# A decoder layer on one core: separate tiles for the raw weights of the first batch, and feed-forward weights and residual rows issued on GpSimd's queue

## The chip, the core and the metric

The kernel runs on one core of a Trainium2 chip. The core has a matrix engine (TensorE, PE), a vector engine (VectorE, DVE), an activation engine (ScalarE, ACT), a general engine (GpSimd, POOL) and SyncE (SP), which here only issues DMAs. Each engine works through its own instructions in order and waits on semaphores for the others. A DMA is issued by an engine and is in that engine's order: what stands behind an issue that waits, waits too. Data lie in SBUF (128 partitions), sums of matmuls in eight PSUM banks, inputs and outputs in DRAM. The metric is the device time of one launch in microseconds (us); the median of the runs is what counts. One further execution was recorded by the hardware profiler.

## The reference: what is computed

One pre-norm decoder layer in fp32, with batch B = 4, T = 512 rows and D = 512 columns: attention with 16 heads of 128, cross attention with a given context, and a feed-forward part of width 1365 with ternary weights. Cut to what matters:

```python
# attention: x is the normed input; att mixes the 128 features of a head
q = (x @ Wq + bq).reshape(Bx, Tx, N_Q, N_HEADS)      # k, v in the same way
q = jnp.transpose(q, (0, 3, 2, 1))
k = jnp.transpose(k, (0, 3, 1, 2))
v = jnp.transpose(v, (0, 3, 2, 1))
att = jax.nn.softmax(q @ k / math.sqrt(N_K), axis=-1)
y = jnp.transpose(att @ v, (0, 2, 1, 3)).reshape(Bx, -1, N_V * N_HEADS)
x_1 = x_0 + y @ Wo + bo
# cross attention: 8 heads of 64 rows, keys and values are the context
x_2 = x_1 + gamma * (softmax(q_heads^T k_heads * scale) applied to v_heads)
# feed-forward, w1, w3, w2 replaced by ternary values
s = jnp.mean(jnp.abs(w)); q = jnp.clip(jnp.round(w / s), -1.0, 1.0) * s
x_3 = x_2 + (silu(n @ w1q.T) * (n @ w3q.T)) @ w2q.T
```

The product `q @ k` contracts over the 512 rows, so a head's scores are a 128x128 matrix.

## The kernel before

**Algebra and stages.** The scores are formed from the Gram matrix G of the normed input (`gram_upper`, `pg`), so that per head only products of 512x512 matrices with weights are left. The 16 heads fall into HG = 4 rounds j of NG = 4 heads. In a round, `u` is the input times a quarter of Wo (matmuls `pu`), `y` is G times Wk (`py`), `m` is Wv times `u` (`pm`), and `scores` makes `sc` from `y` and Wq, its row maximum `nmax` on DVE, and `e`, the softmax numerators, on ACT. `e` is scaled on DVE, turned by PE in the next round (`pe`, `turned`), multiplied with `m` (`po`, `output`) and added to four accumulators `acc`, which hold the residual rows. After round 3 these are stored to DRAM as `x_a`.

There are three stages. The first batch (lines 671 to 743) loads the raw weights from the inputs. The loop over batches 1 to 3 (752 to 778) does the same with weights that the first batch has prepared. The feed-forward stage follows (795 to 889).

**Exact products.** A matmul in plain fp32 is one path (`products_f32`). The other (`products`) splits both operands into a high part `h`, a low part `l` and a difference `d` (three tiles, called Tri) and sums a chain of `h` and `l` products and a chain of `d` products; the two PSUM banks are joined on DVE by `total`. In the first batch, `FIRST` says from which round on a kind of weight uses the split path: `o` from 2, `k` from 1, `v` never.

**Weights of the first batch.** `first_weights(n, j, ...)` loads, for a kind n of `o`, `k`, `v`, `q` and a round j, four raw chunks of 128x512 (256 KB each) on SP, and for `k`, `v`, `q` one tile `last`; DVE then gates each chunk in place (a bias row is put in by a small DMA on POOL). The gate is a number made from an earlier result (`gate_of`), so that the order of the work is kept. `keep_weights` makes the parts on DVE (`h` at line 253, `l` at 255, `d` at 258) and stores each part to DRAM (`kept`, line 244) by a DMA on POOL's queue. Raw chunks of `o` and `q` share the tag `raw` with 7 buffers; raw chunks of `k` and `v` and all parts of `o` lie in the pool `a_w` with 18 buffers; the parts of `k` and `v` share `part` with 12.

**Weights of the later batches.** `weights(n, b, j)` loads the kept parts on SP into the same pool `a_w`. In batch 1 a part `d` that was not kept is made on DVE and stored on POOL. The pool `a_w` is open from the start, beside the pool `first`; the pools of the cross attention (`c_x`, `c_in`, `c_p`, `c_pt`) are opened after `first` is closed and lie in its space.

**Side work.** While PE works through the rounds of batches 1 to 3, two generators give out one step at a time at each `tick`. `cross` does the cross attention of the batch before: it reads `x_a` back (`cs` for the moments, `cx` for the values), loads `keys`, and stores `x_c`; its DMAs are on SP, those of the last batch on POOL. `quantize` does the ternary weights: it loads 35 pieces (`abs`, up to 128x512) into the pool `a_stage` of two buffers and sums their absolute values on DVE (line 498), and later loads the same pieces again (`tern`), makes ternary values and stores them to DRAM as `t_w`. For all of this, `staged` and the store at line 525 use `load`, which is SP's queue. At the end of round 3 of the first batch the two stage buffers are held (`held_0`, `held_1`, line 740) until the first two `y` of that round are there.

**What sets the order.** The program text does not fix the order of an engine's instructions: a scheduler places them engine by engine. So where a DMA stands on its queue, and where a reduce stands on DVE, follow from the scheduler and from which buffers come free when. DMAs of a queue take eight semaphores in turn.

Of the kernel before, what the change touches and what calls it, by code (L numbers as in the profile page):

```python
# [37 lines left out]
def decoder_layer_kernel(  # L38
# [91 lines left out]
    def apool(name, bufs):  # L130
        return apools.enter_context(tc.tile_pool(name=name, bufs=bufs))

    x3p, xnp, g3p, u3p, wp = (
        apool("a_x3", 12), apool("a_xn", 4), apool("a_g3", 1), apool("a_u3", 12), apool("a_w", 18)
    )
    yp, stp, tp = apool("a_y", 5), apool("a_stage", 2), apool("a_t", 3)
    ep, mp, accp = apool("a_e", 1), apool("a_m", 4), apool("a_acc", 4)
    bo_bc = g3p.tile([P, D], F32, name="bo_bc")
# [39 lines left out]
    def load(dst, src):  # L178
        nc.sync.dma_start(dst, src)
        return dst  # L180

    def wtile(name, dt=F32R):
        return wp.tile([P, GW], dt, tag="w", name=name)

    w_of = {"q": wq, "k": wk, "v": wv}

    def heads(t):
# [23 lines left out]
    def first_weights(n, j, first, gate):  # L211

        if n != "o":
            last = first.tile([P, GW], F32, tag="last", bufs=2, name=f"{n}_last_{j}")
            load(heads(last), of_heads(w_of[n][:, D - 1 : D, :], j).to_broadcast([P, NG, DH]))
        chunks = []
        for k in range(KC):
            name = f"{n}_raw_{j}_{k}"
            if n in "oq":
                t = first.tile([P, GW], F32, tag="raw", bufs=7, name=name)  # L220
            else:
                t = wtile(name, F32)
            if n == "o":
                load(t, by_group(wo[j * T : (j + 1) * T, :], k))
            else:
                load(heads(t), of_heads(w_of[n][:, ts(k, P), :], j))
                nc.vector.scalar_tensor_tensor(t, t, gate[0], last, ALU.mult, ALU.subtract)
                if k == KC - 1:
                    bias = bqkv[:, ts(KINDS.index(n), GW)].rearrange("(o g) c -> g o c", o=1)
                    nc.gpsimd.dma_start(heads(t[P - 1 :, :]), of_heads(bias, j))  # L230
            chunks.append(t)
        return chunks

    def keep_weights(n, j, chunks, first, gate):


        def part(p, k):
            name = f"{n}_{p}_{j}_{k}"
            if n == "o":
                return wtile(name)  # L240
            return first.tile([P, GW], F32R, tag="part", bufs=12, name=name)

        def keep(name, tile):
            nc.gpsimd.dma_start(name[ts(k, P), :], tile)

        tris = []
        for k, t in enumerate(chunks):
            if n == "q":
                keep(kept_q[j], t)
                continue  # L250
            tri = Tri(part("h", k), part("l", k), part("d", k) if exact(n, 0, j) else None)
            h, l = tri.h.bitcast(F32), tri.l.bitcast(F32)
            nc.vector.tensor_scalar(tri.h, t, gate[1], None, ALU.mult)
            keep(kept[n, j, "h"], h)
            nc.vector.scalar_tensor_tensor(tri.l, h, -S, t, ALU.mult, ALU.add)
            keep(kept[n, j, "l"], l)
            if tri.d is not None:
                nc.vector.tensor_tensor(tri.d, l, h, ALU.subtract)
                keep(kept[n, j, "d"], tri.d.bitcast(F32))
            tris.append(tri)  # L260
        return tris

    def weights(n, b, j):
        if n == "q":
            return [load(wtile(f"q_{b}_{j}_{k}", F32), kept_q[j][ts(k, P), :]) for k in range(KC)]
        tris = []
        for k in range(KC):
            tri = Tri(*(wtile(f"{n}{p}_{b}_{j}_{k}") for p in "hld"))
            make = b == 1 and not exact(n, 0, j)
            for p in "hl" if make else "hld":  # L270
                load(getattr(tri, p).bitcast(F32), kept[n, j, p][ts(k, P), :])
            if make:
                nc.vector.tensor_tensor(
                    tri.d, tri.l.bitcast(F32), tri.h.bitcast(F32), ALU.subtract
                )
# [187 lines left out]
    def output(b, j, eT, ms, accs):  # L463
        for g in range(NG):
            po = bank(f"po_{b}_{j}_{g}")
            nc.tensor.matmul(po, lhsT=eT[:, g, :], rhs=ms[g], start=True, stop=True)  # L466
            scale = (S if exact("o", b, j) else 1.0) * (S if exact("v", b, j) else 1.0)
            nc.vector.scalar_tensor_tensor(accs[g], po, scale, accs[g], ALU.mult, ALU.add)  # L468
            if j == HG - 1:
                (nc.gpsimd if b == B - 1 else nc.sync).dma_start(by_group(x_a[b], g), accs[g])  # L470


    third = (HID + 2) // 3
# [9 lines left out]

    def staged(src, name):
        r, n = src.shape
        return load(stp.tile([P, 512], F32, tag="stage", name=name)[:r, :n], src)

    def quantize_steps(name):

# [27 lines left out]
        for i, (src, t) in enumerate(pieces):  # L517
            piece = staged(src, f"tern_{name}_{i}")
            r, n = t.shape
            above = stp.tile([P, 512], BF16, tag="above", name=f"above_{name}_{i}")  # L520
            nc.vector.tensor_scalar(above[:r, :n], piece, s[:r, 0:1], None, ALU.is_gt)
            nc.vector.scalar_tensor_tensor(
                piece, piece, s[:r, 1:2], above[:r, :n], ALU.is_lt, ALU.subtract
            )
            load(t, piece)
            yield

    def quantize():
# [142 lines left out]
    for j in range(HG):  # L671
# [77 lines left out]
        cpools.enter_context(tc.tile_pool(name=n, bufs=k, side="right"))  # L749
        for n, k in (("c_x", 3), ("c_in", 2), ("c_p", 4), ("c_pt", 2))  # L750
    ]
    for b in range(1, B):
        G = gram_upper(b, xs)
        waiting[2] = turned(*waiting[:3])
        output(*waiting)
        side = Side(cross(b - 1, *cpool), CROSS_STEPS, TICKS + 6)

        def tick():
            quant.tick()
            side.tick()  # L760

        g3 = gram_rest(b, G)
        for j in range(HG):
            u3 = values_out(b, j, x3, weights("o", b, j), tick)
            if j > 0:
                waiting[2] = turned(*waiting[:3])
            ys = keys_of(b, j, g3, weights("k", b, j), tick)
# [7 lines left out]
            ms = values_of(b, j, weights("v", b, j), u3, tick)  # L775
            e = scores(b, j, weights("q", b, j), ys)
            waiting = [b, j, e, ms, accs]
        side.rest()
    waiting[2] = turned(*waiting[:3])
    output(*waiting)  # L780
    quant.rest()
    apools.close()


# [151 lines left out]
```

## Time and profile before

| what | us |
| --- | --- |
| median of 3 runs | 1235.23 (1233.06 to 1236.63) |
| the profiled execution | 1231.67 |
| its span, first to last instruction | 1229.4 |
| PE busy | 1184.3 |
| DVE busy | 777.5 |
| ACT busy | 448.5 |
| POOL busy | 140.9 |
| end of `sc` of round 3 of the first batch, from the span's start | 215.4 |
| mean granted clock of PE | 0.992 of full |

The profile has a page and views that can be asked for. The page gives busy times and, in 40 slices of the span, the busy tenths of each engine (9 is 90% or more), PE's granted clock in tenths, and the share in which the 16 DMA engines were busy. The view of waits lists, for an engine, the line and tile that waited, what released it, the total in us, how often, and the longest. The timeline gives start, duration, engine, line, operation, output<-input, and in brackets the idle time before with its releaser. The view by stretches gives each engine's busy time in a window with the count of instructions in brackets, then the granted clock, the DMA share and GB/s. SPq and POOLq are the DMA issues of SP and POOL. DMA issues with their time from issue to landing:

```profile
kept_kh<-k_h POOLq DMA_DIRECT2D x16, 256.0 KB, 6.6
kept_vh<-v_h POOLq DMA_DIRECT2D x16, 256.0 KB, 5.0
kept_q<-q_raw POOLq DMA_DIRECT2D x16, 256.0 KB, 2.9
k_raw<-in_wk_dram SPq DMA_DIRECT2D x16, 256.0 KB, 8.3
v_raw<-in_wv_dram SPq DMA_DIRECT2D x16, 256.0 KB, 6.5
abs_w<-in_w1t_dram SPq DMA_DIRECT2D x12, 227.5 KB, 3.5
abs_w<-in_w3t_dram SPq DMA_DIRECT2D x12, 227.5 KB, 5.1
x_a<-acc SPq DMA_DIRECT2D x12, 256.0 KB, 2.5
keys<-in_kv_dram POOLq DMA_DIRECT2D x4, 256.0 KB, 3.3
x_a<-acc POOLq DMA_DIRECT2D x4, 256.0 KB, 4.2
cs<-x_a POOLq DMA_DIRECT2D x4, 256.0 KB, 3.0
```

The last column is the median time from issue to landing in us; the rows on POOL for `keys`, `x_a` and `cs` are those of the last batch.

### The profile page before, as it was taken

How to read it: one execution, taken by the hardware profiler on the slowest of the kernel's cores; microseconds unless marked ns; L12 is line 12 of the kernel's file. 1: busy time of each engine (PE TensorE's matmuls, PEld its weight loads, DVE VectorE, ACT ScalarE, POOL GpSimd, SP SyncE). 2: the span in 40 equal slices, each digit the busy share in tenths (PEclk: the TensorE clock that was granted, in tenths of full speed). 3: DMA queues.
4: the chain of work that ended last, by engine and by line, in shares of the span. 5: the costliest groups of instructions: out<-in, count | busy, mean ns of one | idle time of the engine just before them, and what ended most of it. 6: DMA issues, size and time to landing. Idle time of an engine off the chain costs nothing.

```text
span 1229.4 us, 15851 instructions
## 1 busy us (share of the span) xinstructions
PE 1184.3 (96%) x5262; PEld 825.7 (67%) x5262; DVE 777.5 (63%) x1579; ACT 448.5 (36%) x946; POOL 140.9 (11%) x238
## 2 busy tenths in 40 slices
PE   7999889889999999999999999999999999999998
PEld 3456565567776666777676677777667766678786
DVE  6866958587586856666677557485847835634232
ACT  2221212235242433433343334243445826823020
POOL 2533533120000001000000010000001000000000
PEclk9999999889999999999999999999999999999999
DMA  9799897786778686866787696677963120030101
GB/s 286 269 314 319 299 297 258 226 281 228 241 239 286 203 299 232 282 214 231 241 297 243 211 318 226 214 273 266 342 231 113 43 94 9 9 106 6 61 9 52
DMA packets 154137, 257.20 MB, mean 209 GB/s; under 512 B 16068, under 2 KB 59124, under 8 KB 154056
## 3 DMA queue, kind: packets, MB, share of 16 engines
q1 hardware_dynamic: 139272, 208.97, 51.6%
q0 software_dynamic: 14784, 47.22, 10.2%
q8 instruction: 42, 0.69, 0.2%
q14 instruction: 39, 0.32, 0.1%
HBM read 193.22 MB, written 62.91 MB: 208 GB/s over the span
## 4 chain that ended last, share of the span: by engine, by line
PE 80%; DMA 8%; DVE 4%; issue 4%; POOL 1%; ACT 1%; SPq 1%; POOLq 0%; DVEq 0%; ACTq 0%
PE h L851 13%; PE y L878 7%; PE xs L575 5%; PE xo L619 5%; PE xp L106 4%; PE sc L429 4%; PE po L466 4%; PE pg L361 2%; PE pm L320 2%; PE pu L320 1%; PE py_1d L299 1%; PE py_3d L299 1%; DMA abs_w<-in_w1t_dram 1%; PE py L320 1%; PE py_1h L288 1%
## 5 line engine op out<-in xcount | busy, mean ns | idle before, releaser
L851 PE MATMUL h<-fxh,t 128*128 128x512 f32 (+1 forms) x352 | 140.5, 401 | 0.8 <-ACT fxh L116 0.8
L851 PE MATMUL h<-fxl,t 128*128 128x512 f32 (+1 forms) x352 | 138.3, 395 | 0.0
L587 ACT ACTIVATE p<-xs,xnmax 128x512 f32<-128x512 f32 x128 | 87.0, 687 | 80.6 <-DVE xnmax L582 41.3
L581 DVE TENSOR_REDUCE xnmax<-xs 128x1 f32<-128x512 f32 x128 | 84.1, 685 | 30.6 <-PE xs L575 30.6
L851 PEld LDWEIGHTS h<-fxh,t 128*128 128x128 f32 (+1 forms) x352 | 65.1, 185 | 20.0 <-issue 1.5
L851 PEld LDWEIGHTS h<-fxl,t 128*128 128x128 f32 (+1 forms) x352 | 65.1, 185 | 15.7
L575 PE MATMUL xs<-keys,qs 64*128 64x512 f32 x256 | 73.0, 641 | 1.3 <-DVE m L308 1.3
L878 PE MATMUL y<-t,gh 128*128 128x512 f32 (+1 forms) x176 | 69.5, 395 | 0.0
L878 PE MATMUL y<-t,gl 128*128 128x512 f32 (+1 forms) x176 | 68.9, 391 | 0.0
L106 PEld LDWEIGHTS xp<-ident,p 128*128 128x128 f32 x512 | 58.8, 140 | 13.2 <-issue 3.0
L106 PE MATMUL xp<-ident,p 128*128 128x128 f32 x512 | 66.5, 273 | 0.8 <-DVE u L308 0.8
L619 PE MATMUL xo<-pt,vals 128*64 128x512 f32 x256 | 63.3, 599 | 2.4 <-ACT pt L109 2.4
L862 DVE SCALAR_TENSOR_TENSOR gf<-h,scales_w,sl 128x512 f32<-128x512 f32 (+1 forms) x44 | 32.9, 748 | 48.3 <-PE h L851 39.9
L109 ACT COPY pt<-xp 128x512 f32<-128x512 f32 x96 | 53.4, 594 | 26.5 <-PE xp L106 26.5
L466 PE MATMUL po<-m,eT 128*128 128x512 f32 x128 | 60.3, 615 | 2.7 <-ACT eT L109 2.7
L599 DVE TENSOR_SCALAR p<-p,xrden 128x512 f32<-128x512 f32 x128 | 56.4, 483 | 3.3
L320 PE MATMUL pm<-u,v_raw 128*128 128x512 f32 x128 | 55.6, 592 | 0.0
L663 POOL TENSOR_TENSOR acc<-acc,bo_bc 128x512 f32<-128x512 f32 x16 | 21.1, 1338 | 289.9 <-DMA acc<-in_x_dram 238.6
L860 ACT ACTIVATE sl<-h,scales_w 128x512 f32<-128x512 f32 (+1 forms) x44 | 30.2, 688 | 63.1 <-PE h L851 62.9
L468 DVE SCALAR_TENSOR_TENSOR acc<-po,acc 128x512 f32<-128x512 f32 x64 | 42.6, 687 | 15.6 <-PE po L466 15.4
L442 ACT ACTIVATE e<-sc,nmax 128x128 f32<-128x128 f32 x64 | 22.7, 369 | 79.8 <-DVE nmax L438 79.8
L171 ACT ACTIVATE uh<-u 128x512 fp32r<-128x512 f32 x48 | 30.4, 633 | 49.9 <-DVE u L308 49.7
(262 smaller groups left out, 2545.5 us busy)
## 6 DMA issues: line engine op xcount, KB each, us to landing
oh<-kept_oh SPq DMA_DIRECT2D x48, 256.0 KB, 4.7
ol<-kept_ol SPq DMA_DIRECT2D x48, 256.0 KB, 5.0
kh<-kept_kh SPq DMA_DIRECT2D x48, 256.0 KB, 5.0
kl<-kept_kl SPq DMA_DIRECT2D x48, 256.0 KB, 4.7
vh<-kept_vh SPq DMA_DIRECT2D x48, 256.0 KB, 4.5
vl<-kept_vl SPq DMA_DIRECT2D x48, 256.0 KB, 5.1
q<-kept_q SPq DMA_DIRECT2D x48, 256.0 KB, 5.2
kd<-kept_kd SPq DMA_DIRECT2D x44, 256.0 KB, 4.8
```

Source lines behind the costliest of these rows:

```text
L106: nc.tensor.transpose(pt[:, ts(k, P)], src[:, ts(k, P)], ident)
L109: nc.scalar.copy(dst, pv)
L320: nc.tensor.matmul(p, lhsT=lhs(k)[:, ts(i, P)], rhs=rhs(k), start=(k == 0), stop=(k == 3))
L429: nc.tensor.matmul(sc[:, ts(g, DH)], lhsT=w[k][:, ts(g, DH)], rhs=ys[k][:, ts(g, DH)], start=(k == 0), stop=(k == KC - 1),)
L466: nc.tensor.matmul(po, lhsT=eT[:, g, :], rhs=ms[g], start=True, stop=True)
L575: nc.tensor.matmul(sc, lhsT=qs[rows, ts(m, P)], rhs=keys[rows, :], start=True, stop=True)
L581: nc.vector.reduce_max(nmax[:, j : j + 1], scs[j], axis=AX.X)
L587: nc.scalar.activation(p, scs[j], AF.Exp, bias=nmax[:, j : j + 1], scale=xscale, accum_out=den[:, j : j + 1],)
L599: nc.vector.tensor_scalar(ps[j], ps[j], rden[:, j : j + 1], None, ALU.mult)
L619: nc.tensor.matmul(po[rows, :], lhsT=vals[:, l, rows], rhs=pt[j][:, l, :], start=(l == 0), stop=(l == NC - 1),)
L851: nc.tensor.matmul(ph[:r, :], lhsT=t[:, k, i * P : i * P + r], rhs=fxT[j][:, k, :], start=(k == 0 and j == 0), stop=(k == KC - 1 and j == 1),)
L878: nc.tensor.matmul(py, lhsT=g[i][j][:r, ts(c, P)], rhs=t2[:r, i, :], start=(i == 0 and j == 0), stop=(i == NHC - 1 and j == 1),)
```

## The change

Three things are changed. The raw chunks of the first batch get a tag for each kind with four buffers (16 in all), `last` has three buffers, and the parts get places by kind: exact `o` parts `h` and `l` go to the pool `a_u3`, exact `o` parts `d` to four tiles `od`, all parts of `v` to four tiles `vpart`, and `part` with its 12 tiles is left to `k` and to the `o` parts of the first two rounds. The pool `a_w` is opened only after `first` is closed and after the pools of the cross attention, on the right side, with waits for each tile instead of for the whole pool, and is closed before the other pools of attention. And 117 DMAs go from SP's queue to POOL's: the 70 loads of `staged`, the 35 stores of ternary values, and the 12 stores of `x_a` of batches 0 to 2 (those of batch 3 were on POOL before).

```diff
-    x3p, xnp, g3p, u3p, wp = (
-        apool("a_x3", 12), apool("a_xn", 4), apool("a_g3", 1), apool("a_u3", 12), apool("a_w", 18)
-    )
+    x3p, xnp, g3p, u3p = apool("a_x3", 12), apool("a_xn", 4), apool("a_g3", 1), apool("a_u3", 12)
...
-            last = first.tile([P, GW], F32, tag="last", bufs=2, name=f"{n}_last_{j}")
+            last = first.tile([P, GW], F32, tag="last", bufs=3, name=f"{n}_last_{j}")
...
-            if n in "oq":
-                t = first.tile([P, GW], F32, tag="raw", bufs=7, name=name)
-            else:
-                t = wtile(name, F32)
+            t = first.tile([P, GW], F32, tag=f"raw_{n}", bufs=4, name=name)
...
-            if n == "o":
-                return wtile(name)
-            return first.tile([P, GW], F32R, tag="part", bufs=12, name=name)
+            if n == "o" and exact(n, 0, j):
+                if p != "d":
+                    return u3p.tile([P, D], F32R, tag="u3", name=name)
+                tag, bufs = "od", 4
+            else:
+                tag, bufs = ("vpart", 4) if n == "v" else ("part", 12)
+            return first.tile([P, GW], F32R, tag=tag, bufs=bufs, name=name)
...
-    def weights(n, b, j):
+    def weights(n, b, j, wp):
+        def wtile(name, dt=F32R):
+            return wp.tile([P, GW], dt, tag="w", name=name)
...
-                (nc.gpsimd if b == B - 1 else nc.sync).dma_start(by_group(x_a[b], g), accs[g])
+                nc.gpsimd.dma_start(by_group(x_a[b], g), accs[g])
...
     def staged(src, name):
         r, n = src.shape
-        return load(stp.tile([P, 512], F32, tag="stage", name=name)[:r, :n], src)
+        piece = stp.tile([P, 512], F32, tag="stage", name=name)[:r, :n]
+        nc.gpsimd.dma_start(piece, src)
+        return piece
...
-            load(t, piece)
+            nc.gpsimd.dma_start(t, piece)
...
+    wpools = ExitStack()
+    wp = wpools.enter_context(tc.tile_pool(name="a_w", bufs=18, side="right", reuse_waits="tile"))
     for b in range(1, B):
...
-            u3 = values_out(b, j, x3, weights("o", b, j), tick)
+            u3 = values_out(b, j, x3, weights("o", b, j, wp), tick)
...
+    wpools.close()
     apools.close()
```

More of the change, by code (lines that the diff above doesn't have):

```diff
@@ L180, in load @@
         return dst
-    def wtile(name, dt=F32R):
-        return wp.tile([P, GW], dt, tag="w", name=name)
     w_of = {"q": wq, "k": wk, "v": wv}
@@ L763, in decoder_layer_kernel @@
         for j in range(HG):
-            u3 = values_out(b, j, x3, weights("o", b, j), tick)
+            u3 = values_out(b, j, x3, weights("o", b, j, wp), tick)
             if j > 0:
                 waiting[2] = turned(*waiting[:3])
-            ys = keys_of(b, j, g3, weights("k", b, j), tick)
+            ys = keys_of(b, j, g3, weights("k", b, j, wp), tick)
             if j > 0:
@@ L774, in decoder_layer_kernel @@
                 x3 = parts_of(b + 1, xs)
-            ms = values_of(b, j, weights("v", b, j), u3, tick)
-            e = scores(b, j, weights("q", b, j), ys)
+            ms = values_of(b, j, weights("v", b, j, wp), u3, tick)
+            e = scores(b, j, weights("q", b, j, wp), ys)
             waiting = [b, j, e, ms, accs]
```

## The prediction

> **What bounds the kernel now.** I read the page first, to see whether any engine is the bound.
>
> ```profile
> span 1229.4 us, 15851 instructions
> PE 1184.3 (96%) x5262; PEld 825.7 (67%) x5262; DVE 777.5 (63%) x1579; ACT 448.5 (36%) x946; POOL 140.9 (11%) x238
> PE   7999889889999999999999999999999999999998
> PEclk9999999889999999999999999999999999999999
> DMA  9799897786778686866787696677963120030101
> ```
>
> TensorE (PE) is busy 96%: 45 us of idle time is all that better overlap could remove, plus what a lowered clock costs. Both lie in the first quarter: from slice 10 (about 310 us) PE shows 9 throughout and the clock is full. So the table of PE's waits comes next.
>
> ```profile
> PE pg L361 <- DVE xn L338: 8.7, 1, 8.7
> PE pu_2d L299 <- ACT e L442: 5.2, 1, 5.2
> PE py_0h L287 <- DMA kh<-kept_kh: 4.6, 4, 2.2
> PE pe L106 <- DVE e L453: 4.3, 2, 3.3
> PE pu_3d L299 <- ACT e L442: 3.3, 1, 3.3
> ```
>
> The first line is the start and stays. The two `pu` lines belong to the first batch; I look up what made `e` late there in the timeline.
>
> ```profile
> 119.22 0.75 DVE L227 SCALAR_TENSOR_TENSOR k_raw<-k_raw,gate,k_last 128x512 f32<-128x512 f32 x1 [7.72 <-DMA k_raw<-in_wk_dram]
> ...
> 123.84 0.68 DVE L437 TENSOR_REDUCE nmax<-sc 128x4 f32<-128x512 f32 x1
> ...
> 128.13 3.24 PE L299 MATMUL pu_2d<-o_d,xd 128*128 128x512 f32 x7 [5.20 <-ACT e L442]
> ...
> 166.39 0.75 DVE L227 SCALAR_TENSOR_TENSOR k_raw<-k_raw,gate,k_last 128x512 f32<-128x512 f32 x1 [9.31 <-DMA k_raw<-in_wk_dram]
> ...
> 174.41 0.68 DVE L437 TENSOR_REDUCE nmax<-sc 128x4 f32<-128x512 f32 x1
> ```
>
> The scores `sc` were done at 113.6 (start 109.87, 3.73 long), but their maximum `nmax` ran at 123.84: it stands on VectorE (DVE) behind work on `k_raw`, and DVE idled 7.72 us for that load. `e` frees the PSUM bank that `pu_2d` waits for. In round j=3 the same happens with 9.31 us. The `k_raw` issues begin at 110.28 and 156.85, behind other kinds of weight on SP's queue. The third place is the transition to batch 1:
>
> ```profile
> 224.33 0.68 DVE L437 TENSOR_REDUCE nmax<-sc 128x4 f32<-128x512 f32 x1
> ...
> 227.49 1.08 PE L106 MATMUL pe<-ident,e 128*128 128x128 f32 x4 [3.33 <-DVE e L453]
> ```
>
> Here ten reduces of `abs_w` stand before `nmax`, and their loads come in pairs, since the stage pool has two buffers. Last, the table by stretches (the figure after POOL is the granted clock):
>
> ```profile
> 120.00:130.00 10.00, 4.80 (x17) 3.58 (x17) 8.68 (x19) 4.24 (x12) 3.40 (x7) 0.89 0.75 237
> 220.00:230.00 10.00, 5.95 (x26) 4.33 (x25) 4.62 (x15) 3.91 (x14) 0.54 (x1) 0.83 0.71 223
> 250.00:260.00 10.00, 7.30 (x18) 4.94 (x19) 9.69 (x19) 4.51 (x8) 2.17 (x3) 0.70 0.72 235
> ```
>
> Each stall is followed by a lowered clock. A stretch of 10 us at clock c loses 10(1−c).
>
> **First batch: raw tiles per kind.** Stalls between the start and 215.4 (end of `sc` of j=3) sum to 12.4 us: 5.2 + 3.3, and 3.9 in small ones of the same table cut to this stretch (0.9 for `k_l`, 0.9 for `u`, 0.8 for `gate` and four below 0.6), most of them again for parts of `k`, which come earlier now. The clock lost 1.1 (0.89) + 0.6 (0.94) + 0.5 (0.95) + 1.2 (0.88) = 3.4 us.
> - j=2 and j=3: in the new instruction order `k_raw` of the next round is issued as soon as its own four tiles are read, half a round early, so DVE no longer idles for it. What `nmax` stands behind is then `v_raw`, whose load waits for the previous `pm`, done about 110; it lands 6.5 us after issue, 116. Then `nmax` at about 117 instead of 123.84, `e` at about 121 (3.4 us of table load and four exponentials, as at 125.28 to 127.96), and PE wants the bank at 122.9 (128.13 − 5.20). Gain 5.2. In j=3 `nmax` falls from 174.41 to about 162: gain 3.3.
> - j=1 pays. Two `k_raw` loads for j=2 stand on SP ahead of `v_raw` for j=1, and wait for the parts of `k`; `v_raw` is issued about 69, lands about 76, and `nmax`, at 64.51 before, goes behind four `v_raw` operations (4 × 0.75) to about 77, `e` to about 81. PE wants that bank at about 82. Margin 1 us; from there each us late is a us of stall. I take 1 us of stall, bounds 0 and 5 (the j=2 stall moved here).
> - `v` now has 4 part tiles for 8 parts: the fifth waits for the store of the first, 5.0 us (row of `kept_vh` on POOL). DVE is in order, so `q_raw` and `nmax` would be queued behind it; the totals of `u` and the scaling of `e` lie between and cover it. Bounds 0 and 8 us over four rounds (four times the 5.0 less 3 us of such work).
> - The extra `last` tile and `o` parts in other pools cost nothing by themselves: the waits on them were on tiles read 40 us earlier.
> - Bytes: 57.9 MB in 200 us before, DMA share 0.86 on average. About 2 MB of batch 1's first weights go later; 55.9 MB in 184 us is 304 GB/s, and at the 335 GB/s per full share seen (288/0.86) a share of 0.91. Stretches of 10 us at 1.03 and 1.07 occur before (80 to 90, 110 to 120), so it fits, but queueing returns some of the gain: I take 1 us, bounds 0 and 6.
>
> First batch: 12.4 + 3.4 − 1 − 1 = 13.8, so 14 us gained; with all bad bounds (5 + 8 + 6) it is 3 us lost.
>
> **Transition: feed-forward weights on POOL, weight pool opened later.** 117 DMAs leave SP (70 loads, 35 stores, 12 residual stores). On SP they cost issue time of 0.33 to 0.44 us each, about 45 us over 1000 us of a queue that isn't the bound; on POOL 0.54 us each, 63 us on an engine busy 140.9. The gain sought is that weights no longer queue behind a stalled `abs_w`. But `keys` of the cross attention now stands on SP ahead of six of the eight `oh`/`ol` loads, and waits for the whole first pool, to T0 (end of `sc` j=3). After T0 there are 8.9 (`pg`) + 5 (`pe`, `po`, `gt`) us of PE work before the first `pu`, then 11.2 us of it; the last `oh`/`ol` pair waits for `pg`'s reads, is issued at about T0+10, lands 5 us later, and is wanted at T0+18 (after those 13.9 and the stall of 4.1 below). Covered, by 3 us; without that stall it would wait about 1 us itself.
> - All 12 `abs_w` reduces now stand ahead of `nmax`, ten before. The first pair is free to load 19 us before T0 (its tiles are held until `y` of j=3 is copied, 196.22 before, with T0 at 215.4). Six pairs, each a landing L and 1.4 us of reduces, then 3.8 us for `nmax`, `e` and its scaling; PE asks at T0+8.9. The stall is 6(L+1.4) + 3.8 − 19 − 8.9 = 6L − 15.7. POOL never loaded `abs_w`: its nearest rows are `keys` 3.3, `cs` 3.0, `cx` 2.9 (quiet queues) and, upwards, `kept_kh` 6.6 in the busy first batch. I take 3.3, the same shape from an input: 4.1 us, against 3.33 + 0.72 = 4.05 now. Bounds 2.9 (1.7 us) and 6.6 (23.9 us).
> - `kh` loads: still behind `cs` and `cx`, which now wait for a POOL store of 4.2 us instead of 2.5; but fewer transfers stand on SP. I estimate 3 us of stall against 4.1. Net gain of the transition: 1 us; bounds +6 and −20.
>
> The page "SBUF — State Buffer" of the Trainium skill (section "SBUF: two separate sides") says that a GpSimd DMA waits for descriptors while DVE runs in a fast two-port mode, 620 ns becoming 3100. This speaks against the move. The trace has stores on POOL of 5.0 to 6.6 us among DVE work and 2.9 for `kept_q`, which is compatible. By the page, 2.5 us more for six pairs would add about 15 us; the rows I use come from the feed-forward stage, where DVE is less busy, so they say little on this.
>
> **Later batches and feed-forward.** From 320 us to the end all stalls of PE together are about 13 us, 1.6 of them from DMAs; the queue move can win at most that. It can lose where `cs` waits for a residual row on POOL behind feed-forward pieces and holds weights: covered by 18 weight buffers; 0, bounds +1.6 and −5.
>
> **Sum.** 14 + 1 + 0 = 15 us: span 1229.4 to 1214.4. The profiled run took 1231.67 (2.3 around the span), 3.6 below the median of 1235.23; taken off the median, 1220.
>
> **Rivals.**
> A. *The stalls only move.* `v_raw` becomes what `k_raw` was, `v`'s four tiles serialize DVE, and the queues are full at 0.91. For it: the 1 us margin in j=1. Against: the wait for `v_raw` before was 1.31 us in j=2. Price: the 5 us of j=1, 4 of the 8 for `v`, 3 of queueing out of 16: gain 4, time 1231.
> B. *The `abs_w` chain on POOL becomes the wait at the transition.* Place: DVE's queue ahead of `nmax` of j=3. It eats the other gains from 6L − 15.7 = 4.05 + 15, L = 5.8. For it: all twelve reduces are ahead, only two buffers, POOL rows of 5 to 6.6 in the first batch, and `abs_w` of w3 took 5.1 even on SP. Against: SP stands still at `keys` in that stretch, so the chain has the DMA engines nearly alone. At L = 8.3 (the slowest row, `k_raw`) the stall is 34, less 4 now, less the 14 and 2 us of other gains: 14 slower, 1249.
> C. *It doesn't do what it says:* SP is held at `keys` instead, and weights arrive as late as before while the first batch stays DMA-bound. 1235.
>
> **How the numbers follow.** Forecast 0.55, A 0.15, B 0.27, C 0.03. About 0.3% (3.7 us) is what a measurement of this kernel tells from no change. Faster: 0.55 and 0.09 of A; same: 0.06 of A and 0.02 of C; slower: the rest, 0.28. The forecast's own range is 1208 (all stalls and 6 us of the transition gone, and a little of the lowered clock) to 1229. The wide range reaches into B as far as 1246, with 1 in 10 beyond it and 1 in 10 below 1208.
>
> **What would show it.** Right: no wait of `pu_2d` and `pu_3d` on `e`, no idle DVE before `k_raw` in j=2 and j=3, `sc` of j=3 ending about 201, a clock over 0.95 in the first batch. Wrong: a new wait of `py_1d` on `e`, DVE idle before `v_h` on a `kept_vh` store, or `pe` waiting more than 10 us with `abs_w` landings over 5 us on POOL. A new stall of `pu_0` on `oh` would say that `keys` holds SP longer than I read it.

## The result, and the profile after

The changed kernel takes 1298.18 us in the median (1295.5 to 1300.71), against 1234.61 for the kernel before in the same comparison: a ratio of 1.0514, with an interval of 1.0486 to 1.0541. The prediction was 1220 us, with a range up to 1246. The change is slower by 63.6 us, more than the 14 us at which rival B, the slow one, was priced.

The profiled execution took 1297.42 us. First the page of the changed kernel: busy times, then the busy tenths of PE and its clock in 40 slices.

```profile
span 1295.6 us, 15874 instructions
PE 1209.5 (93%) x5262; PEld 837.3 (65%) x5262; DVE 779.9 (60%) x1579; ACT 448.7 (35%) x946; POOL 208.8 (16%) x355
PE   7989899799978999997889999997998899999998
PEclk9998899999989999998989999998999899999999
```

PE does the same 5262 matmuls, yet it is idle for 86.1 us (1295.6 − 1209.5) where it was idle for 45.1, and busy for 25 us more: the lowered clock now also shows in slices 12, 19, 21, 28 and 32, counted from 1 (from about 356 us on). Before, everything from slice 11 on was full. So the loss isn't in the first batch and the transition, where I had looked for gains and losses, but later. The ends of the `sc` groups on the timelines cut the span into three stages:

| stage | before | after | difference |
| --- | --- | --- | --- |
| first batch: start to the end of `sc` of round 3 | 215.5 | 217.9 | +2.4 |
| batches 1 to 3: from there to the end of the last `sc` | 691.9 | 745.5 | +53.6 |
| feed-forward stage: the rest | 322.0 | 332.2 | +10.2 |

The view of waits for PE in the changed kernel (total, times, longest):

```profile
PE po L465 <- DVE y L307: 15.9, 3, 7.2
PE py_2h L286 <- DVE u L307: 10.4, 2, 7.3
PE xs L576 <- ACT e L441: 9.1, 2, 4.6
...
PE xs L576 <- DVE qs L100: 8.2, 1, 8.2
PE pu_2d L298 <- DVE v_l L251: 5.7, 1, 5.7
...
PE pe L106 <- DVE e L452: 2.6, 2, 1.7
PE py_1d L298 <- ACT e L441: 2.6, 1, 2.6
```

`pu_3d` on `e` (3.3 before) is gone from the table, as predicted; `pe` has fallen to 2.6, where the prediction kept it at 4.1. The first three lines are new (`py_2h` on `u` was 0.4), and lie mostly in batches 1 to 3.

The view of waits cut to batches 1 to 3 says which way the loss goes. The last row sums PE's waits during which DVE itself stood for the load of a feed-forward piece; load_sp is the run below with the pieces' loads back on SP.

| PE in batches 1 to 3, us | before | changed | load_sp |
| --- | --- | --- | --- |
| idle until a DMA landed | 5.5 | 5.4 | 6.5 |
| idle until DVE or ACT was done | 10.0 | 42.9 | 7.8 |
| of these, while DVE stood for a piece | 5.6 | 33.2 | 0.3 |

So PE waits for weights no longer than before. What grew, by 32.9 us, is its waiting for DVE and ACT, and seven waits with DVE standing for a piece make up 33.2 of the 42.9 us. The other 20.9 of the 53.6 us are busy time, at a granted clock of 0.97 instead of 0.99.

One of the two waits of `py_2h`, in the timeline of batch 2:

```profile
603.20 0.55 POOL L486 DMA_DIRECT2D tern_w<-in_w3t_dram  x1 [4.59 <-DMA t_w<-tern_w]
...
609.50 0.46 DVE L522 TENSOR_SCALAR above_w<-tern_w,scales_w 128x455 bf16<-128x455 f32 x1 [7.57 <-DMA tern_w<-in_w3t_dram]
...
610.94 0.68 DVE L307 SCALAR_TENSOR_TENSOR u<-pu_2t,pu_2d 128x512 f32<-128x512 f32 x1
...
611.67 0.79 PE L286 MATMUL py_2h<-kh,gh 128*128 128x512 f32 x1 [7.30 <-DVE u L307]
```

Read it from the top. POOL waits 4.59 us for the store of an earlier piece to land, since the stage pool has two buffers, and only then issues the load. DVE, which is in order, has already come to that piece, and stands 7.57 us for it. Behind it stands `u`, the total that empties a PSUM bank; PE, which needs the bank, stands 7.30 us. The other long waits have the same head: DVE stands 6.03 us at 379.82 and PE 5.03 at 382.20 (`po`); 7.58 at 879.97 and 7.25 at 883.18 (`po`). At these three the load itself needed 4.8 to 6.3 us from issue to DVE's operation. Each is followed by a lowered clock, as the table by stretches shows for two of them (the figure after POOL is the granted clock):

```profile
600.00:625.00 25.00, 17.70 (x75) 12.70 (x74) 15.20 (x32) 8.14 (x18) 5.34 (x9) 0.80 0.62 211
875.00:900.00 25.00, 17.75 (x68) 11.45 (x67) 13.74 (x25) 3.98 (x9) 5.99 (x11) 0.86 0.49 166
```

In the median the loads do not land later after their issue than they did on SP, where the trace has the landing of about half of them; the stores of the pieces do. The issue rows after, and then before (last column: us to landing):

```profile
tern_w<-in_w1t_dram POOLq DMA_DIRECT2D x12, 227.5 KB, 3.5
tern_w<-in_w3t_dram POOLq DMA_DIRECT2D x12, 227.5 KB, 3.7
t_w<-tern_w POOLq DMA_DIRECT2D x24, 227.5 KB, 3.2
```

```profile
tern_w<-in_w1t_dram SPq DMA_DIRECT2D x12, 227.5 KB, 4.1
tern_w<-in_w3t_dram SPq DMA_DIRECT2D x12, 227.5 KB, 5.5
t_w<-tern_w SPq DMA_DIRECT2D x24, 227.5 KB, 2.5
```

What differs more is where DVE's work on a piece stands. Between the first ternary operation on a piece (`above_w`) and that on the piece two on, whose load needs its buffer, the trace has for w3 196 DVE instructions before (summed over ten pairs) and 124 after; for w2 (nine pairs) 176 and 131. The scheduler packs the pieces closer once their loads are on POOL. And DVE comes to them sooner: from the issue of a ternary load to the moment at which DVE is ready for it, the median is 4.8 us before and 2.6 after.

In the first batch, round 2 stalls as before, for a new reason. SP, DVE and PE on the timeline, and then the issue row of `v_raw`, which had 6.5 before:

```profile
108.86 5.13 SPq L177 DMA_DIRECT2D o_raw<-in_wo_dram  x4
116.25 0.38 SPq L177 DMA_DIRECT2D k_last<-in_wk_dram  x1
117.38 0.70 SPq L177 DMA_DIRECT2D k_raw<-in_wk_dram  x1
118.17 5.92 SPq L177 DMA_DIRECT2D v_raw<-in_wv_dram  x4
...
129.31 0.75 DVE L219 SCALAR_TENSOR_TENSOR v_raw<-v_raw,gate,v_last 128x512 f32<-128x512 f32 x1 [4.70 <-DMA v_raw<-in_wv_dram]
...
133.43 0.68 DVE L436 TENSOR_REDUCE nmax<-sc 128x4 f32<-128x512 f32 x1
...
137.79 3.35 PE L298 MATMUL pu_2d<-o_d,xd 128*128 128x512 f32 x7 [5.72 <-DVE v_l L251]
```

```profile
v_raw<-in_wv_dram SPq DMA_DIRECT2D x16, 256.0 KB, 9.9
```

`v_raw` of round 2 is issued at 118.17, behind loads for round 3 (`o_raw`, `k_last`, one `k_raw`) that wait for DVE to be done with round 2's own tiles. The larger part of the delay is another: the tiles of `v_raw` are free only when `pm` of round 1 has read them, and `pm` ran until 119.10 (110.04 before), since round 1 had lost 8 us. In round 3, where nothing stands ahead of them, the four loads go between 168.36 and 170.93 with `pm` ending at 170.90; by this, the first could have gone at about 116.6 here, an estimate, and the queue held it for 1.6 us. From its issue to DVE's operation the first load then needed 11.1 us, with the DMA engines full (share 1.00 from 110 to 130). So DVE stands for `v_raw`, and `nmax` and `e` are late once more.

The feed-forward stage: SP and POOL in the changed kernel, and then in the kernel before.

```profile
972.22 0.32 SPq L544 DMA_DIRECT2D x_c<-cx  x1
972.89 6.74 SPq L177 DMA_DIRECT2D t<-t_w  x11
...
985.98 1.64 POOL L544 DMA_DIRECT2D cs<-x_a  x3 [8.16 <-DMA t<-t_w]
```

```profile
886.10 26.37 SPq L179 DMA_DIRECT2D t<-t_w  x26
916.15 0.32 SPq L543 DMA_DIRECT2D x_c<-cx  x1
...
926.51 1.63 POOL L543 DMA_DIRECT2D cs<-x_a  x3 [4.75 <-DMA x_a<-acc]
```

The 11 loads of w2's ternary weights stand behind the last `x_c` store now, and fall together with the last residual rows' way through DRAM: `cs` waits 8.16 us instead of 4.75, then `qs` is late, and PE's `xs` waits 8.2 us.

### The profile page after: what moved, and what is told of

The parts are those of the page before. It is cut to its first block, busy times and chain, and to the rows that moved or that the text cites. A ratio compares the mean times of both kernels' runs of the same rounds, so it can differ in the third digit from the quotient of the medians.

```text
span 1295.6 us, 15874 instructions
## 1 busy us (share of the span) xinstructions
PE 1209.5 (93%) x5262; PEld 837.3 (65%) x5262; DVE 779.9 (60%) x1579; ACT 448.7 (35%) x946; POOL 208.8 (16%) x355
## 5 line engine op out<-in xcount | busy, mean ns | idle before, releaser
L576 PE MATMUL xs<-keys,qs 64*128 64x512 f32 x256 | 81.0, 666 | 17.9 <-ACT e L441 9.1
L465 PE MATMUL po<-m,eT 128*128 128x512 f32 x128 | 63.6, 638 | 18.9 <-DVE y L307 15.9
L855 PEld LDWEIGHTS h<-fxl,t 128*128 128x128 f32 (+1 forms) x352 | 65.2, 185 | 15.7
L866 DVE SCALAR_TENSOR_TENSOR gf<-h,scales_w,sl 128x512 f32<-128x512 f32 (+1 forms) x44 | 32.9, 747 | 47.5 <-PE h L855 40.0
L526 POOL DMA_DIRECT2D t_w<-tern_w x35 | 19.8, 567 | 233.8 <-DVE xrden L598 93.2
L465 PEld LDWEIGHTS po<-m,eT 128*128 128x128 f32 x128 | 24.4, 200 | 47.9 <-issue 21.4
L441 ACT ACTIVATE e<-sc,nmax 128x128 f32<-128x128 f32 x64 | 22.7, 369 | 92.8 <-DVE nmax L437 86.1
```

What stands on the lines that cost most here:

```text
L576: nc.tensor.matmul(sc, lhsT=qs[rows, ts(m, P)], rhs=keys[rows, :], start=True, stop=True)
L855: nc.tensor.matmul(ph[:r, :], lhsT=t[:, k, i * P : i * P + r], rhs=fxT[j][:, k, :], start=(k == 0 and j == 0), stop=(k == KC - 1 and j == 1),)
L866: nc.vector.scalar_tensor_tensor(gf[:r, :], hs[1][:r, :], scales["w3"][:r, 2:3], sl[:r, :], ALU.mult, ALU.mult)
```

## The experiments

All are single edits of the changed kernel unless said otherwise; the stages are cut as above (first batch / batches 1 to 3 / feed-forward). "Stood" is DVE's idle time in the whole kernel that ended on an `abs_w` or `tern_w` load.

| run | median | ratio to before, interval | stages | stood |
| --- | --- | --- | --- | --- |
| tiles_only | 1245.09 | 1.0090 (1.0075 to 1.0105) | 218.3 / 690.6 / 333.1 | 46 |
| queue_only | 1290.53 | 1.0476 (1.0448 to 1.0504) | 219.5 / 745.9 / 322.3 | 96 |
| quant_back | 1247.33 | 1.0106 (1.0087 to 1.0126) | 216.8 / 693.2 / 332.1 | 44 |
| xa_back | 1292.59 | 1.0480 (1.0465 to 1.0496) | 217.7 / 740.5 / 332.3 | 99 |
| late_pool | 1251.64 | 1.0138 (1.0100 to 1.0175) | 221.1 / 695.0 / 331.6 | 47 |
| v_pool | 1252.34 | 1.0149 (1.0108 to 1.0190) | 224.4 / 695.6 / 332.4 | 42 |
| store_sp | 1282.76 | 1.0394 (1.0359 to 1.0429) | 217.8 / 730.2 / 332.8 | 70 |
| stage3 | 1279.23 | 1.0359 (1.0318 to 1.0399) | 219.0 / 736.7 / 322.2 | 60 |
| v8_f2 | 1219.83 | 0.9902 (0.9885 to 0.9918) | 205.4 / 690.3 / 322.0 | 42 |
| no_tern | 1303.06 | 1.0581 (1.0557 to 1.0605) | 218.4 / 749.1 / 332.5 | 65 |
| no_dve | 1294.55 | 1.0478 (1.0429 to 1.0526) | 216.8 / 742.8 / 333.2 | 0 |
| load_sp | 1249.02 | 1.0112 (1.0073 to 1.0151) | 218.5 / 697.3 / 332.7 | 45 |
| paced | 1333.91 | 1.0808 (1.0779 to 1.0837) | 217.3 / 776.3 / 335.5 | 161 |
| best_paced | 1296.32 | 1.0507 (1.0472 to 1.0542) | 203.7 / 760.7 / 323.3 | 159 |

Before itself stood 49, the changed kernel 96.

### Which part of the change costs what

tiles_only: all 117 DMAs back on SP (`staged`, the store of `t_w`, and `x_a` as before).

```diff
-                nc.gpsimd.dma_start(by_group(x_a[b], g), accs[g])
+                (nc.gpsimd if b == B - 1 else nc.sync).dma_start(by_group(x_a[b], g), accs[g])
...
-        piece = stp.tile([P, 512], F32, tag="stage", name=name)[:r, :n]
-        nc.gpsimd.dma_start(piece, src)
-        return piece
+        return load(stp.tile([P, 512], F32, tag="stage", name=name)[:r, :n], src)
...
-            nc.gpsimd.dma_start(t, piece)
+            load(t, piece)
```

> The changed kernel with all 117 DMAs put back on SP's queue: the tiles and the pool order of the change alone. Theory 1 (the feed-forward pieces on POOL stop DVE in batches 1 to 3): first batch as in the changed kernel (sc of round 3 ends at about 218 us), batches 1 to 3 as before, 1238 us, between 1228 and 1246. Theory 2 (the weight pool opened late and the few v parts are the loss): 1270 or more. Theory 3 (residual rows on POOL hold cs and SP): as theory 1.

queue_only: the kernel before, with these same lines as the change has them.

> The kernel before with only the 117 DMAs moved to POOL. Theory 1: 1290 us, between 1275 and 1305, with above_w and sums_w on DVE waiting about 80 us for tern_w and abs_w loads in batches 1 to 3 as in the changed kernel, against some 38 before. Theory 2: 1240 or less. Theory 3: 1290, but then with the putting back of the residual rows alone most of it must vanish.

quant_back puts back only the second and third of these places; xa_back only the first.

> The changed kernel with the 70 loads and 35 stores of the feed-forward pieces back on SP; the residual rows stay on POOL. Theory 1: 1245 us, between 1235 and 1255. Theory 3: 1285 or more. Theory 2: 1275 or more.

> The changed kernel with only the 12 residual stores of batches 0 to 2 back on SP; the feed-forward pieces stay on POOL. Theory 1: 1290 us, between 1280 and 1300. Theory 3: 1250 or less. Theory 2: 1290 to 1298.

Theory 1 holds for where the loss comes from: the queue move alone costs 56.5 us on the kernel before, 54.0 of them in batches 1 to 3; the pieces put back win 51 us of the changed kernel, the residual rows 5.6, which is hardly clear of the intervals. The tiles and the pool order cost 11 us, in the feed-forward stage and the first batch (batches 1 to 3 are 1.3 shorter than before). Theories 2 and 3 fall.

### Why the pieces cost so much on POOL

store_sp: the stores of `t_w` back on SP.

```diff
-            nc.gpsimd.dma_start(t, piece)
+            load(t, piece)
```

> The changed kernel with only the 35 stores of ternary values back on SP; the 70 loads stay on POOL. Theory S (on POOL each store is held behind the next load, which itself waits for the store before, so the chain through two buffers is a round trip for every piece): at least half of the 51 us that the pieces cost goes, 1272 us or less. Rival (loads on POOL are late by themselves, or DVE's new order): 1288 or more.

stage3: a third stage buffer.

```diff
-    yp, stp, tp = apool("a_y", 5), apool("a_stage", 2), apool("a_t", 3)
+    yp, stp, tp = apool("a_y", 5), apool("a_stage", 3), apool("a_t", 3)
...
-            last = first.tile([P, GW], F32, tag="last", bufs=3, name=f"{n}_last_{j}")
+            last = first.tile([P, GW], F32, tag="last", bufs=2, name=f"{n}_last_{j}")
...
-            above = stp.tile([P, 512], BF16, tag="above", name=f"above_{name}_{i}")
+            above = stp.tile([P, 512], BF16, tag="above", bufs=2, name=f"above_{name}_{i}")
...
-    wp = wpools.enter_context(tc.tile_pool(name="a_w", bufs=18, side="right", reuse_waits="tile"))
+    wp = wpools.enter_context(tc.tile_pool(name="a_w", bufs=17, side="right", reuse_waits="tile"))
```

> The changed kernel with three stage buffers instead of two (room for it: one buffer less for last and one for the weight pool). Theory R (the ring of two buffers makes every load wait for a store's landing, and DVE waits for the load): DVE's waits on tern_w and abs_w fall by more than half, 1270 us or less. Rival (it is the issue and landing on POOL, not the ring): 1288 or more.

Both miss on either side: they win 15 and 19 us, and 10 of the 19 are in the feed-forward stage, where the shifted pools gave back the 332 to 322. In batches 1 to 3 the shorter chain wins 15.3 and the third buffer 8.8 of 53.6 us. Chain and ring are part of the loss, less than half of it each.

load_sp: only the 70 loads back on SP.

```diff
-        piece = stp.tile([P, 512], F32, tag="stage", name=name)[:r, :n]
-        nc.gpsimd.dma_start(piece, src)
-        return piece
+        return load(stp.tile([P, 512], F32, tag="stage", name=name)[:r, :n], src)
```

> The changed kernel with the 70 loads of the feed-forward pieces back on SP, the 35 stores and the residual rows on POOL. If the loads on POOL are what lets the scheduler place the pieces closely on DVE (theory D's cause), most of the loss goes: 1260 or less. If the stores' landing on POOL is the larger part of the chain, 1275 or more.

With the loads alone on SP, batches 1 to 3 take 697.3 us, though the stores stay on POOL and the ring is unchanged: 48 of the 54 us are gone. DVE stands 45 us, close to before, w3's distance on DVE is 197 again, and the median from issue to DVE's being ready is 4.1 us. PE's idle time with DVE standing at a piece falls from 33.2 to 0.3 us (table above). The loads on POOL are the cause.

no_tern leaves out the two DVE operations of each piece, no_dve the sum of absolute values as well.

```diff
-            above = stp.tile([P, 512], BF16, tag="above", name=f"above_{name}_{i}")
-            nc.vector.tensor_scalar(above[:r, :n], piece, s[:r, 0:1], None, ALU.is_gt)
-            nc.vector.scalar_tensor_tensor(
-                piece, piece, s[:r, 1:2], above[:r, :n], ALU.is_lt, ALU.subtract
-            )
```

> The changed kernel without the two DVE operations that make a piece ternary (line 522 and 523): the pieces are loaded and stored by the same DMAs on POOL, but nothing on DVE waits for the second loads. Theory D (the loss is DVE, in order, standing at a piece that has not landed, with PE's evictions behind it): 51 us of loss fall by at least half, 1272 us or less, with no long wait of po or py_2h left except where abs_w is waited for. Rival (the DMAs on POOL slow other transfers): 1288 or more.

```diff
-            nc.vector.tensor_reduce(
-                sums[: piece.shape[0], i : i + 1],
-                piece,
-                AX.X,
-                ALU.add,
-                apply_absolute_value=True,
-            )
```

> The changed kernel without any DVE work on the feed-forward pieces: neither the sums of absolute values nor the two operations that make a piece ternary; all 105 DMAs of the pieces stay on POOL and still wait for each other's buffers. Theory D (the loss is DVE, in order, standing at a piece that has not landed; the run without the ternary operations alone let the scheduler pack the sums of w3 and w2 into batch 1, and stood there instead): no wait of PE above 2.5 us between the first sc of batch 1 and the last sc, these 15 rounds take about 685 us as before, total 1250 us, between 1240 and 1258. Rival (the DMAs on POOL slow other transfers or hold residual rows and weights): 1285 or more.

Theory D missed in both: the time stayed, and by the number the rival came true. The reason is in where the pieces went. Their last load is at 893 us in the changed kernel, at 445 in no_tern and at 435 in no_dve: with less DVE work between them, the scheduler ends all 70 in batch 1. In no_tern DVE still stood 65 us there, now at `abs_w`. In no_dve it stood at none, and PE's waits are of another kind:

```profile
PE py_0h L286 <- DMA kh<-kept_kh: 24.2, 5, 18.6
...
PE pu_3h L287 <- DMA ol<-kept_ol: 7.1, 1, 7.1
```

And SP's queue there, from 225 to 460 us:

```profile
SPq L177 <- DMA kept_vd<-vd: 49.8, 10, 12.5
SPq L177 <- DMA x_a<-acc: 22.4, 2, 22.1
```

The stores of residual rows and of `d` parts now stand on POOL among pieces that wait for each other's buffers, and SP, which needs those stores landed before it may load into their tiles, holds the weights. That is the rival's way, and in no_dve it is real: PE is idle 39.4 us there until a DMA lands, in batches 1 to 3. In the changed kernel this is 5.4 us, so it isn't the way of the loss there. These two runs don't test theory D as meant: they trade one victim for another. They do show something by their later part. In no_tern no piece is loaded after 445 us, while residual rows, tiles and pools are those of the change: its nine rounds from the `sc` that ends at 454.0 to the last one take 513.5 us. The same nine rounds take 512.9 before and 557.6 in the changed kernel. So in these rounds the loss comes with the pieces, and not with rows, tiles or pools.

paced: in `staged`, a small DVE copy from the latest total (`latest`, set in `total`) into the buffer, ahead of the load.

```diff
         piece = stp.tile([P, 512], F32, tag="stage", name=name)[:r, :n]
+        nc.vector.tensor_copy(piece[:, 0:1], latest[0][:r, 0:1])
         nc.gpsimd.dma_start(piece, src)
```

> The changed kernel, all 117 DMAs on POOL, with one small DVE copy (one column of the latest total of PE's products into the piece's buffer) ahead of each of the 70 loads: a load can't be issued, and its DVE work not be placed, before the main work has come as far as its step. Theory Q (the loss is that loads on POOL let the pieces be placed close together on DVE and POOL, closer than a store and a load through two buffers take): the 51 us of the queue move go, 1250 us or less, no wait of PE over 2.5 us behind a piece. Rival (the two-buffer chain or POOL's landing costs by itself, wherever the pieces stand): 1275 or more.

best_paced: the same on v8_f2 (below), with the residual rows on SP.

> The run with eight raw tiles for v and w2's pool last (1219.8 us with all pieces on SP), with the 105 DMAs of the pieces on POOL and the same small DVE copy ahead of each load; residual rows on SP. Theory Q: pacing removes the queue's cost, so it stands at 1220 us, between 1213 and 1228; whether POOL then is better than SP for the pieces is open. Rival: 1260 or more.

Theory Q falls in this form: both runs lie far above its numbers. The pieces are spread out (259 DVE instructions for w3 instead of 124), and it is slower by 36 us. The copy lets each load go only when DVE has come that far, and DVE is then ready for the piece 2.6 us later in the median, while the load takes 4.5 us; so it stands for nearly every piece. The copy thus adds a wait of its own, and the runs don't show that the rival is right:

```profile
DVE sums_w L503 <- DMA abs_w<-in_w2t_dram: 32.8, 10, 5.8
DVE sums_w L503 <- DMA abs_w<-in_w3t_dram: 29.7, 10, 5.2
DVE above_w L526 <- DMA tern_w<-in_w3t_dram: 26.0, 11, 5.9
```

This is DVE's view of waits in paced between 300 and 960 us; the changed kernel has 21.5 in 7 for the third. So more distance between pieces alone doesn't help; how long before DVE's operation the load is issued fits better, though no run varied it alone. Where DVE's work on the pieces is kept, batches 1 to 3 roughly follow the time that DVE stood: 42 to 47 us stood give 690 to 697 us (before, with 49, 691.9), 60 and 70 give 736.7 and 730.2, 96 gives 745.5 and 745.9, 99 (xa_back) 740.5, 159 (best_paced) 760.7 and 161 776.3. The time stood isn't the price by itself: in load_sp DVE stood 37 us within these batches, and PE was idle beside it for 0.3 us only. It costs where an eviction stands behind it that PE waits for.

### The pool order and the first batch

late_pool: the kernel before, with the weight pool opened as in the change and the first batch's 18 shared buffers in `first`.

```diff
-                t = wtile(name, F32)
+                t = first.tile([P, GW], F32, tag="w", bufs=18, name=name)
...
-                return wtile(name)
+                return first.tile([P, GW], F32R, tag="w", bufs=18, name=name)
```

> The kernel before with only the pool order of the change: the later batches' weight pool is opened after the first batch's pool is closed, and the first batch keeps its 18 shared buffers in its own pool. Queues as before. Theory P (the place of the weight pool moves the loads of the feed-forward weights t behind the last residual work): the feed-forward stage, from the end of the last sc to the end, grows from 322 us to about 332 with a wait of xs on qs of 8 us, first batch as before (sc of round 3 ends at about 216): 1242 us, between 1236 and 1248. Rival (the 10 us of that stage come from the tiles per kind): 1235, stage 322.

The feed-forward stage of 331.6 us with a wait of `xs` on `qs` of 8.0 us bears out theory P. The total is above the range, since the first batch also grew to 221.1; why was not followed up.

v_pool: on tiles_only, the raw loads of `v` on POOL.

```diff
-                load(heads(t), of_heads(w_of[n][:, ts(k, P), :], j))
+                queue = nc.gpsimd if n == "v" else nc.sync
+                queue.dma_start(heads(t), of_heads(w_of[n][:, ts(k, P), :], j))
```

> The run with the tiles of the change alone (all feed-forward pieces and residual rows on SP), and the 16 raw loads of v in the first batch issued on POOL instead of SP. Theory V (in the changed kernel v_raw stands on SP behind prefetches of the next round for o and k, which wait for DVE): v_raw is issued earlier, the wait of pu_2d vanishes, sc of round 3 ends at 209 us or earlier instead of 218, total 1236 or less. Rival (v's four part tiles and the full DMA engines set the first batch): sc of round 3 at 216 or later, total 1243 or more.

Theory V missed: the first batch is longer (224.4). On POOL the loads took 7.9 us to land, and `po` waited 13.5 us once. This gave `v_raw` another queue, but a later issue (76.94 against 64.44 us in round 1, 140.56 against 117.96 in round 2 of tiles_only), so the theory was tried again with buffers.

v8_f2: on tiles_only, eight raw tiles for `v`, and w2's pool opened last.

```diff
-            t = first.tile([P, GW], F32, tag=f"raw_{n}", bufs=4, name=name)
+            t = first.tile([P, GW], F32, tag=f"raw_{n}", bufs=8 if n == "v" else 4, name=name)
...
-                tag, bufs = ("vpart", 4) if n == "v" else ("part", 12)
+                tag, bufs = "part", 12
...
-    f1, fxb, f3, fx, f2, fwk, fg = (
+    f1, fxb, f3, fx, fwk, fg, f2 = (
-        fpool("f_w1", 1), fpool("f_xb", 1), fpool("f_w3", 1), fpool("f_x", 2), fpool("f_w2", 1),
-        fpool("f_work", 2), fpool("f_g", 2 * NHC),
+        fpool("f_w1", 1), fpool("f_xb", 1), fpool("f_w3", 1), fpool("f_x", 2),
+        fpool("f_work", 2), fpool("f_g", 2 * NHC), fpool("f_w2", 1),
```

> The run with the tiles of the change alone (all 117 DMAs on SP), with two edits: eight raw tiles for v instead of four (v parts share the 12 part tiles with k again), and in the feed-forward stage the pool of w2 opened last, so that it lies in the space of the weight pool. Theory V (v_raw is late because its load stands behind prefetches for the next round): v_raw is loaded a round ahead, the waits of pu_2d and py_1d on e vanish, sc of round 3 ends at 210 us or earlier instead of 218; rival (part tiles or full DMA engines): 216 or later. Theory F (the loads of w2's ternary weights wait for tiles that live to the end, and then collide with the residual rows' way through DRAM): the stage after the last sc takes 322 to 324 us instead of 333, without the wait of xs on qs; rival: 330 or more. Both right: 1228 us or less; both wrong: 1243 or more.

Both theories' numbers came true, and the version beats both kernels: 1219.83 us, 1.0% below before. The first batch takes 205.4 us and the last stage 322.0, with no wait of `xs` on `qs`. `v_raw` of round 1 is issued at 37.83 instead of 64.44, and DVE stands 1.8 us for `v_raw` in the first batch where it stood 16.8 in tiles_only, though the loads take as long to land (9.6 against 10.6 us). The second edit above also gives the parts of `v` the 12 shared tiles back, and DVE's 13.9 us of standing for `kept_vh` and `kept_vl` stores are gone too: what each of the two is worth was not separated. Its page and PE's waits:

```profile
span 1217.7 us, 15845 instructions
PE 1183.5 (97%) x5262; PEld 825.0 (68%) x5262; DVE 776.2 (64%) x1579; ACT 449.3 (37%) x946; POOL 143.2 (12%) x238
```

```profile
PE pg L360 <- DVE xn L337: 8.5, 1, 8.5
PE pu_2d L298 <- ACT e L441: 3.5, 1, 3.5
PE pu_0h L287 <- DMA ol<-kept_ol: 2.8, 1, 2.8
```

`py_1d` is gone; `pu_2d`, which the expectation had gone too, falls from 10.3 us (tiles_only) to 3.5.

## Why the prediction was wrong, point by point

- **Later batches: "0, bounds +1.6 and −5".** This is the step that failed: 53.6 us lie there. I read that PE was not waiting for DMAs there and that POOL had room, and asked only who waits for `cs`. I didn't ask what DVE does when a piece comes late, though the pieces' operations stand in DVE's order between PE's evictions, and DVE stood 49 us at them already before, with little harm (5.6 us of PE's idle time in these batches). I used the new instruction order for the first batch and the transition, but not for DVE in these batches, where the pieces stand closer together (196 to 124 for w3). That the loads' queue is the cause is shown (load_sp, queue_only). That in the changed kernel the way goes over DVE is shown by PE's waits: those for DMAs stayed (5.5 and 5.4 us), those for DVE and ACT grew from 10.0 to 42.9. How much is the two-buffer ring, how much the shorter lead and how much the slower stores was not separated: no run changed the queue and kept the order.
- **Rival B** named the right parts, the pieces' chain on POOL with two buffers, but at the wrong place. At the transition the twelve reduces are ahead of `nmax`, as read, and `pe` waits 1.66 us there, not 4.1: `abs_w` of w1 landed in 2.9 us, for which the formula 6L − 15.7 gives 1.7. So the formula fits, with L at its lower bound, and the transition brought a little more than the 1 us put down: from the end of `sc` of round 3 to that of the next round it takes 64.4 us, 68.1 before. (The rival's price counts 2 us of other gains at the transition where the sum has 1.)
- **First batch, 14 us gained:** lost 2.4. The term that was mis-sized is the landing of `v_raw`: put at 6.5 us, it was 9.9 in the median with the DMA engines full, and DVE stood 16.9 us for it. In round 1 the loads were issued between 64.98 and 71.89 and took 8.8 us and more, so `nmax` ran at 81.41, not at about 77, behind the `k_raw` loads of round 2 as read; the round lost 2.6 us at `py_1d`, 3.6 at `po` and part of its clock, where I had put 1 us. Round 2 didn't gain: its `v_raw` waits for the previous `pm`, as read, but that was done at 119.10 and not at "about 110", the queue held the load for some 1.6 us more, and it landed 11 us after its issue. The four part tiles of `v`, put within 0 and 8 us and at nothing in the sum, made DVE stand 14.8 us for `kept_vh` and `kept_vl` stores, one of the signs of being wrong. Round 3 took 43.4 us instead of 50.6, the gain of 3.3 that I had worked out for it and more. Rival A was right here, and v8_f2, where both kinds of standing are gone, bears it out.
- **Pools:** the prediction has "`o` parts in other pools cost nothing by themselves", and no term for the later opening of `a_w`. The feed-forward stage, which no step looked at, grew by 10 us. late_pool and v8_f2 show that the order of the pools, and with it w2's place in memory, is what costs it.
- **The Trainium skill's rule** on the page "SBUF — State Buffer" (section "SBUF: two separate sides"), that a GpSimd DMA is starved of descriptors while DVE runs in a fast mode, spoke against the move, and the move was bad; but not for that reason as far as these runs show, since the ternary loads of w1 and w3 landed in 3.5 and 3.7 us on POOL against 4.1 and 5.5 on SP. The stores did land later, which would fit it: 4.2 us against 2.5 for the 12 of `x_a` that moved, 3.2 against 2.5 for ternary values. No run here shows whether that is the reason.
- **Residual rows:** put at a small loss within "0, bounds +1.6 and −5"; measured 5.6 us between xa_back and the changed kernel and 2.2 between quant_back and tiles_only, with intervals that overlap in both pairs.

## What to carry to other kernels

A DMA that is moved to a free queue changes the order of every engine that consumes it: compare the lead between the load's issue and its consumer's place in that engine's order, not only the queue's load and the landing time. An operation off the critical path that stands in an in-order engine's stream among evictions is on the path as soon as its data is late; here 48 us more of DVE standing came with 54 us more in batches 1 to 3. Ask too what stands behind the late operation: the 49 us that DVE stood before cost PE little. And when tiles get new pools, look at every later pool that inherits their space: a buffer that lives longer delays loads far away.

## What the runs showed of the hardware that was not expected

A 227.5 KB load issued on POOL landed in the median no later than on SP (3.5 against 4.1 us, 3.7 against 5.5), while 256 KB stores of residual rows took 4.2 against 2.5. One stall of 7 us on PE costs more than itself: the granted clock was 0.71 from 604.4 to 611.6 us, while PE stood 7.30 us, and 0.53 in the 6.3 us after it, in which PE was busy throughout, about 3 us more by the same rule as in the prediction (6.3 × 0.47).
